# Batches of eight edge groups in a graph layer's gathers, the last chunk of the last group first

## The chip, the cores and the metric

The kernel runs on one core of a Trainium2 chip. The metric is the device time of one execution in microseconds (us); a profiled execution gives the rows of the trace. Engines: PE is TensorE (matmuls; PEld is its weight loads), DVE is VectorE, ACT is ScalarE, POOL is GpSimd, SP is SyncE.

## The reference

A graph layer over 12,500 nodes of 128 features and 200,000 edges, which come sorted by destination. Cut to what matters:

```python
hn = relu(layernorm(x))
w = edge_weight / max(segment_sum(edge_weight, dst), EPS)[dst]
feat = relu(hn @ W_pool + b_pool)
neigh = segment_max(feat[src] * w[:, None], dst)          # 0 for nodes without edges
h = relu(rownorm(hn @ W1_self + neigh @ W1_neigh + b1))
neigh2 = segment_sum(h[src] * w[:, None], dst) / max(deg, 1)
out = x + relu(h @ W2_self + neigh2 @ W2_neigh + b2)
```

So each edge needs a row of `feat` in the first pass and a row of `h` in the second, picked by its source node.

## The kernel before

The edges are cut into NG = 391 groups of G = 512, each of four chunks of P = 128 rows (the last group has 320 edges, three chunks). One chunk is one indirect DMA that GpSimd issues: `gather` (L502, the instruction at L507) makes four of them for a group, each picks 128 rows of 512 bytes out of a table in DRAM and puts them into one quarter of a buffer of 128 x 512 floats.

After a first stage that builds `feat_d` (its first 17 groups are gathered from x and treated apart), **pass 1** is one loop over the groups (L866 on; the gather is called at L877). In step i PE transposes the four chunks of group i into PSUM tile `pm` (L896), DVE multiplies them by the weights `gs` (L940), a step later it scans along the edges for the maximum (L911, with `kt` telling where a destination begins), copies (L933, L936) and picks the columns that end a destination (`sel`, L922). PE turns these back (`pr`, L952) and a product with `sel` (`pn`, L961) puts them into a window of nodes. About every four groups 128 nodes are complete; the node stages (L742 on) make h of them with PE, DVE and ACT and store it to `h_d`.

**Pass 2** (the loop after L1050, the gather at L1052) needs no transposes: DVE compares the edges' places (L996) and weighs them into `s` (L1001), PE multiplies each chunk by its part of `s` into `pa` (L1008, the chunks in reversed order, so the last chunk is read first), and DVE adds `pa` into the window of nodes (L1013). Each group has one L940 in pass 1 and one L1013 in pass 2. Nodes are finished about every four groups again. Groups 0 to 2 of this pass are gathered ahead.

The buffers come from `buffer`. At first there is a ring of 18 (some lent by other tables), then one of 14, and from group 113 of pass 1 on, and in all of pass 2, a ring of RING + MORE = 11 buffers called `full` (gt_98 to gt_108 in the listings). So a gather into a buffer waits until PE has read the group that stood in it before, which is eleven groups back in the ring of eleven. This wait is on PE's semaphore. Each gather has also a wait on its own lane of DMA completions (DMASW0 to DMASW7, eight lanes). The order of the instructions on each engine is the order of the code (a manual schedule); GpSimd does nearly nothing but gathers in the two passes. SP's queue loads `gs` for each group and `kt` for each four, DVE and ACT read the windows' places into registers for eight groups (BL = 8) at a time.

Of the kernel before, what the change touches and what calls it, by code (L numbers as in the profile page):

```python
# [18 lines left out]
P = 128  # L19
# [24 lines left out]
ADDED = PART_AT[-1] + PART  # L44
SCRATCH = 8192
MORE = 3


@with_exitstack
def gnn_kernel(ctx, tc, x, src, dst, ew, w_pool, b_pool, w1s, w1n, b1, w2s, w2n, b2, out):  # L50
# [20 lines left out]
    NG = GF + 1  # L71
# [7 lines left out]
    feat_d = dram.tile([NP, D], F32, name="feat_d")  # L79
    h_d = dram.tile([NP, D], F32, name="h_d")  # L80
# [40 lines left out]

    full = [gp.tile([P, Q, D], F32, name=f"gt{k}") for k in range(RING + MORE)]
    ring = full[:RING]
# [8 lines left out]
    def buffer(g, wide):  # L132
        if not wide:
            return full[g % len(full)]
        if WIDE <= g < WIDE + 3:
            k = g - WIDE
            return (work(f"f{k}").rearrange("p (q d) -> p q d", d=D) if k < 2 else ewT[:, 1])
        h = g if g < WIDE else g - 3
        if h < LESS:
            return ring[h % WIDE]  # L140
        return mid[(h - LESS) % MID] if h < LEAST else full[(h - LEAST) % len(full)]
# [36 lines left out]
    def strided(a, t, n):  # L178

        t0 = t - t % n  # L180
        return a[:, t0 * P:(t0 + n) * P].rearrange("d (p q) -> d q p", q=n)[:, t % n, :]
# [71 lines left out]
    def work(name, n=G, dtype=F32):  # L253
        return rp.tile([P, n], dtype, name=f"r_{name}")
# [242 lines left out]
    def edges_of(g):  # L497

        ne = G if g < GF else TAIL
        return *divmod(g, P), ne, [(j, min(P, ne - j * P)) for j in range(-(-ne // P))]  # L500

    def gather(gt, table_d, g, only=None, last=None):  # L502

        t, r, ne, chunks = edges_of(g)
        limit = {} if last is None else dict(bounds_check=last, oob_is_err=False)
        for j, k in chunks if only is None else chunks[only:only + 1]:
            nc.gpsimd.indirect_dma_start(  # L507
                out=gt[:k, j, :], out_offset=None, in_=table_d[:, :],
                in_offset=bass.IndirectOffsetOnAxis(ap=srcT[:k, t, j, r:r + 1], axis=0), **limit)
        return gt  # L510


    gts = {}
    raws = {}

    def raw_stats(r):
        mv = rp.tile([P, Q, 2], F32, name="raw_mv", bufs=3)
        for q in range(Q):
            st = rp.tile([P, 6], F32, name="raw_st", bufs=2)
            nc.vector.bn_stats(st, gts[r][:, q, :])  # L520
            nc.vector.bn_aggr(mv[:, q, :], st)  # L521
        rstd = rp.tile([P, Q], F32, name="raw_rstd", bufs=3)
        nc.scalar.activation(rstd, mv[:, :, 1], AF.Sqrt, bias=eps)
        raws[r] = mv, rstd
# [80 lines left out]
    for i in range(len(groups) + 3):  # L605
# [50 lines left out]
        while raw_chunks and 1 <= i <= 17:  # L656
            r, j = raw_chunks[0]
            if r >= WIDE - NT and i < 15 or r > WIDE - 3 and i < 17 or i < 9 and len(raw_chunks) <= Q * FIRST - 3 * i:
                break
            gts[r] = gather(buffer(r, True), x, r, only=j)  # L660
            raw_chunks.pop(0)
# [5 lines left out]
        k = i - len(groups)  # L667
# [29 lines left out]
    def pairs_of(g):  # L697

        t, r, ne, _ = edges_of(g)
        return t, r, ne, [(j, min(P, ne // 2 - j * P)) for j in range(-(-ne // (2 * P)))]  # L700
# [4 lines left out]
    def wide2(t):  # L705
        return Q if t < NF // Q * Q else 1
# [18 lines left out]
    def window_at(engine, g):  # L725

        if g % BL == 0 or engine not in held:
            lo = g // BL * BL
            _, held[engine] = nc.values_load_multi_w_load_instructions(
                bases[0:1, lo:min(lo + BL, NG)], [engine], min_val=0, max_val=N - 1,  # L730
                skip_runtime_bounds_check_because="destinations of edges are nodes, as the gathers have it")
        return held[engine][g % BL]
# [13 lines left out]
    def linear_own(po, t, self_w, n=1):  # L746
        nc.tensor.matmul(po, strided(turned_to[self_w], t, n), W[self_w], start=True, stop=False)
# [36 lines left out]
    def x_rows(wk, t, n, bufs):  # L784
        xr = wk.tile([P, n, D], F32, name=f"xr{n}", bufs=bufs)
        if n > 1:
            nc.sync.dma_start(in_runs(xr, n), runs(x, t, n, n))
        else:
            (q, p, view), = rows_of(x, t, 1)
            nc.sync.dma_start(xr[:p], view)  # L790
        return xr

    def nodes2(wk, ps, t, n, nT, xr):

        po = linear(ps, t, n, nT, "2s", "2n", b2_all)
        yield
        (q, p, view), = rows_of(out, t, 1)
        if t % n == 0:
            together["o"] = wk.tile([P, n, D], F32, name=f"o{n}", bufs=2)
        all_o = together["o"]  # L800
        o, xr = all_o[:p, t % n, :], xr[:p, t % n, :]
        nc.vector.scalar_tensor_tensor(o, po[:p, :], 0.0, xr, op0=OP.max, op1=OP.add)
        if n == 1:
            nc.sync.dma_start(view, all_o[:p])
        elif t % n == n - 1:
            nc.sync.dma_start(runs(out, t + 1 - n, n, n), in_runs(all_o, n))

    def stages(steps):
        for _ in steps:
            pass  # L810


    with tc.manual_schedule(), tc.tile_pool(name="ew", bufs=3) as wk, \
# [26 lines left out]
        def due(k):  # L840

            return i - k if 0 <= i - k < NG else None
# [23 lines left out]
        for i in range(max(turn) + 6):  # L866
# [7 lines left out]
            if i % KEPT == 0 and i and i + 2 < NG:  # L874
                keep_rows(i + 2, keep_tile())
            if FIRST <= i < NG:
                gts[i] = gather(buffer(i, True), feat_d, i)  # L877

            if i + 1 < NG:
                weight_rows(i + 1, wk.tile([P, G], F32, name="gs"))  # L880
# [12 lines left out]
            elif i < NG:  # L893
                gt = gts.pop(i)
# [5 lines left out]
            g = due(3)  # L900
            if g is not None:
                t, r, ne, chunks = pairs_of(g)
# [4 lines left out]
            g = due(1)  # L907
# [6 lines left out]
            if due(3) is not None:  # L914
                t, r, _, chunks = pairs_of(due(3))
# [31 lines left out]
            g = due(2)  # L947
# [7 lines left out]
            g = due(4)  # L955
            if g is not None:
                chunks = pairs_of(g)[3]
# [19 lines left out]
        i = NG  # L977
        side_step()
        for e in range(EARLY):
            gather(early[e], h_d[:(HI - LATE) * P], e, last=(HI - LATE) * P - 1)  # L980


    with tc.manual_schedule(), tc.tile_pool(name="ew2", bufs=3) as wk, \
# [10 lines left out]
        def places(g):  # L994
            t, r, _, _ = edges_of(g)
            nc.vector.tensor_tensor(hit, iota, locT[:, t, :, r:r + 1].to_broadcast([P, Q, PART]), OP.is_equal)  # L996

        def weighted(g):
            t, r, _, _ = edges_of(g)
            ss[g] = wk.tile([P, Q, PART], F32, name="s")  # L1000
            nc.vector.tensor_tensor(ss[g], hit, w2T[:, t, :, r:r + 1].to_broadcast([P, Q, PART]), OP.mult)  # L1001

        def window_product(g):
            chunks = edges_of(g)[3]
            pas[g] = ps.tile([P, ADDED], F32, name="pa", bufs=3)
            gt, s = gts.pop(g), ss.pop(g)
            for j, k in reversed(chunks):
                nc.tensor.matmul(pas[g][:, PART_AT[j]:PART_AT[j] + PART], gt[:k, j, :], s[:k, j, :],  # L1008
                                 start=j == len(chunks) - 1, stop=j == 0, skip_group_check=True)

        def window_add(g, at):
            n = ADDED if g < GF else PART_AT[len(edges_of(g)[3]) - 1] + PART
            nc.vector.tensor_tensor(agg2[:, bass.ds(at, n)], pas.pop(g)[:, :n], agg2[:, bass.ds(at, n)], OP.add)  # L1013
# [35 lines left out]
        first_groups = early_groups()  # L1049
        for i in range(max(turn) + 2):  # L1050
            if EARLY <= i < NG:
                gts[i] = gather(buffer(i, False), h_d, i)  # L1052
                places(i)
            if EARLY <= i < NG:
                weighted(i)
            if i + 4 in turn:
                n = turn[i + 4]
                if n % wide2(n) == 0:
                    xr = x_rows(wk, n, wide2(n), 2)
                xrs[n] = xr  # L1060
            if late is not None:
                stages(late)
                late = None
            if i in turn:
                n = turn[i]
                late = nodes2(wk, ps, n, wide2(n), strided(agg2, n, wide2(n)), xrs.pop(n))
                next(late)
            g = i - 1
            if EARLY <= g < NG:
                window_product(g)  # L1070
            if i >= EARLY and i % 2:
                next(first_groups, None)
            if i == NG - 1:
                for n in (HI - 2, HI - 1):
                    own[n] = flip[:, 0] if n % 2 else ps.tile([P, Q, D], F32, name="pl", bufs=1)[:, 0]
                    linear_own(own[n], n, "2s")
            g = i - 2
            if EARLY <= g < NG:
                window_add(g, window_at(mybir.EngineType.DVE, g))
# [18 lines left out]
    with tc.If(flag > 0):  # L1098
        with tc.tile_pool(name="gt", bufs=1) as tp, tc.tile_pool(name="gw", bufs=2) as wk, \
# [10 lines left out]
            for t0, n in node_groups():  # L1110
                c = slice(t0 * P, (t0 + n) * P)
                k = n * P
# [89 lines left out]
```

## Time and profile before

| | |
|---|---|
| three runs | 4612.95, 4617.0, 4617.24 us |
| median | 4617.0 us |
| profiled execution | 4650.7 us, its span 4648.7 us |
| mean granted clock of PE | 0.527 |
| gathers from `feat_d` into gt, 944 ns each | 1303 |
| gathers from `h_d` into gt, 944 ns each | 1551 |

A row of a table by stretches gives from:to and length in us, then for each engine (PE, PEld, DVE, ACT, POOL) the busy time and the number of instructions, the granted clock, the DMA engines' busy share and GB/s; of a single line of the kernel it gives only that line's engine. A row of the timeline gives start, duration, engine, line, operation, and in brackets the engine's idle time before it and what ended it; "issue" is time in which it waited for nothing that the profile shows, "remote" is a releaser that the profile cannot name. A row of waits gives total, times and longest.

### The profile page before, as it was taken

What the parts mean: (1) busy time and instruction counts of PE and PEld (TensorE: products, weight loads), DVE (VectorE), ACT (ScalarE), POOL (GpSimd) and SP (SyncE); (2) the same over time, 40 slices, a digit from 0 to 9 for tenths busy, and PEclk for the clock granted to TensorE, in tenths of its full rate; (3) what the DMA queues carried; (4) which work ended last, traced back from release to release, by engine and by line L of the source; (5) the groups of instructions that cost most, each with busy time, mean ns of one, the idle gap of its engine ahead of it and who ended that gap; (6) DMA issues with size and microseconds to landing.
All of it is one profiled execution on the core that took longest, in us unless ns stands there. A gap on an engine that the chain in (4) does not pass through costs nothing.

```text
span 4648.7 us, 32678 instructions
## 1 busy us (share of the span) xinstructions
PE 1995.1 (43%) x8700; PEld 1817.3 (39%) x8700; DVE 1741.8 (37%) x5165; ACT 416.0 (9%) x1509; POOL 2953.3 (64%) x3143
## 2 busy tenths in 40 slices
PE   3654543444444444444453344334334333334334
PEld 2444433443434343433342334333334333333334
DVE  3676655765666566665560111111101111111111
ACT  3531111111111111111110000000000000000000
POOL 5356666666666666666646666666666666666665
PEclk8665555555555555555555555555555555555555
DMA  4333443444444444444431112112111111211111
GB/s 130 109 114 116 126 117 103 125 117 114 118 115 120 115 117 116 119 116 117 113 100 46 47 47 62 51 50 56 50 52 53 51 52 51 55 51 52 53 54 45
DMA packets 196303, 397.11 MB, mean 85 GB/s; under 512 B 60703, under 2 KB 69790, under 8 KB 196112
## 3 DMA queue, kind: packets, MB, share of 16 engines
q0 software_dynamic: 100032, 204.97, 17.3%
q1 hardware_dynamic: 95344, 189.06, 13.2%
q8 instruction: 73, 1.20, 0.1%
q10 hardware_dynamic: 736, 0.92, 0.1%
q14 instruction: 118, 0.97, 0.1%
HBM read 374.96 MB, written 19.77 MB: 85 GB/s over the span
## 4 chain that ended last, share of the span: by engine, by line
another core or an unknown queue 23%; issue 23%; PE 20%; POOL 19%; DVE 13%; DMA 1%; ACT 1%; POOLq 0%; ACTq 0%; DVEq 0%
POOL gt L507 18%; PE pa L1008 5%; PE pm L896 5%; DVE pm L911 4%; PE pn L961 4%; DVE pm L940 2%; PE pr L952 2%; DVE sc L936 1%; DVE sc L933 1%; DMA gt<-h_d,srcT 1%; DVE sel L922 1%; PE pn L743 1%; PE pf L643 1%; PE pn L780 1%
## 5 line engine op out<-in xcount | busy, mean ns | idle before, releaser
L507 POOL DMA_INDIRECT gt<-h_d,srcT x1551 | 1463.9, 944 | 743.6 <-issue 419.6
L507 POOL DMA_INDIRECT gt<-feat_d,srcT x1303 | 1230.0, 944 | 680.5 <-issue 294.5
L1008 PE MATMUL pa<-s,gt 128*128 128x24 f32 x3102 | 685.3, 382 | 734.4 <-remote 561.1
L1008 PEld LDWEIGHTS pa<-s,gt 128*128 128x128 f32 x3102 | 682.0, 330 | 748.7 <-remote 567.8
L1013 DVE TENSOR_TENSOR way<-pa,way 128x41 f32 x391 | 78.0, 199 | 1866.9 <-remote 1323.6
L896 PE MATMUL pm<-ident,gt 128*128 128x128 f32 (+1 forms) x1303 | 349.7, 423 | 521.5 <-issue 314.3
L940 DVE TENSOR_TENSOR pm<-pm,gs 128x512 f32<-128x512 f32 x390 | 271.1, 695 | 694.6 <-remote 529.1
L911 DVE TENSOR_TENSOR_SCAN pm<-kt,carry,pm 128x512 f32<-128x512 bf16 x389 | 496.3, 1276 | 4.0
L961 PEld LDWEIGHTS pn<-sel,rows 128*128 128x128 f32 x1564 | 368.8, 324 | 230.8 <-ACT way L849 128.2
L896 PEld LDWEIGHTS pm<-ident,gt 128*128 128x128 f32 (+1 forms) x1303 | 235.8, 218 | 560.4 <-issue 338.5
L961 PE MATMUL pn<-sel,rows 128*128 128x48 f32 x1564 | 358.2, 377 | 217.4 <-ACT way L849 121.9
L743 PE MATMUL pn<-w_2n,way 128*128 128x128 f32 x192 | 74.4, 491 | 601.3 <-issue 325.9
L743 PEld LDWEIGHTS pn<-w_2n,way 128*128 128x128 f32 x192 | 52.8, 323 | 620.2 <-issue 406.6
L906 ACT ACTIVATE rows<-pr 128x256 f32<-128x256 f32 x392 | 149.7, 383 | 1532.8 <-remote 662.1
L952 PE MATMUL pr<-ident,sc 128*128 128x128 f32 x782 | 241.8, 411 | 8.0 <-issue 3.9
L922 DVE TENSOR_SCALAR sel<-cols,lastT,invT 128x48 f32<-128x48 f32 x782 | 243.6, 312 | 0.0
L933 DVE COPY sc<-pm 128x256 f32<-128x256 f32 x391 | 162.6, 416 | 109.5 <-remote 85.9
L952 PEld LDWEIGHTS pr<-ident,sc 128*128 128x128 f32 x782 | 167.2, 224 | 11.5 <-issue 6.1
L936 DVE COPY_PREDICATED sc<-kt,pm 128x256 f32<-128x256 int16 x389 | 168.5, 433 | 4.9 <-issue 4.9
L507 POOL DMA_INDIRECT w2T<-feat_d,srcT x100 | 94.3, 943 | 105.8 <-DVE raw_mv L521 52.0
L780 PE MATMUL pn<-ident,h 128*128 128x128 f32 x94 | 41.9, 446 | 236.8 <-DVE ss L765 73.0
L780 PEld LDWEIGHTS pn<-ident,h 128*128 128x128 f32 x94 | 17.3, 184 | 270.1 <-issue 217.2
(273 smaller groups left out, 2079.6 us busy)
## 6 DMA issues: line engine op xcount, KB each, us to landing
gs<-in_edge_weight SPq DMA_DIRECT2D x389, 256.0 KB
kt<-keep_d SPq DMA_DIRECT2D x97, 512.0 KB
gt<-h_d,srcT POOLq DMA_INDIRECT x1551
gt<-feat_d,srcT POOLq DMA_INDIRECT x1303
feat_d<-fr SPq DMA_DIRECT2D x24, 256.0 KB
xr<-in_x SPq DMA_DIRECT2D x24, 256.0 KB
out<-o SPq DMA_DIRECT2D x24, 256.0 KB
h_d<-h SPq DMA_DIRECT2D x47, 128.0 KB
```

Source lines behind the costliest of these rows:

```text
L507: nc.gpsimd.indirect_dma_start(out=gt[:k, j, :], out_offset=None, in_=table_d[:, :], in_offset=bass.IndirectOffsetOnAxis(ap=srcT[:k, t, j, ...
L743: nc.tensor.matmul(po, nT, W[neigh_w], start=False, stop=True)
L896: nc.tensor.transpose(pms[i][:, j * P:j * P + k], gt[:k, j, :], ident[:k, :k])
L906: nc.scalar.activation(rws[g][:k, j, :], pr[:k, j, :], AF.Copy)
L911: nc.vector.tensor_tensor_scan(pm[:, :ne], kt[:, :ne], pm[:, :ne], carry, op0=OP.add, op1=OP.max)
L922: nc.vector.tensor_scalar(part, cols[:k, 1, :], lastT[:k, t, j, r:r + 1], invT[:k, t, j, r:r + 1], op0=OP.is_equal, op1=OP.mult)
L933: nc.vector.tensor_copy(sc[:, :ne // 2], two[:, :, 1])
L936: nc.vector.copy_predicated(sc[:, :ne // 2], new[:, :, 1], two[:, :, 0])
L940: nc.vector.tensor_tensor(pms[i][:, :n], rows[:, :n], ws.pop(i)[:, :n], OP.mult)
L952: nc.tensor.transpose(prs[g][:k, j, :], sc[:, j * P:j * P + k], ident)
L961: nc.tensor.matmul(pas[g], rows[:k, j, :], sel[:k, j, :], start=j == 0, stop=j == len(chunks) - 1)
L1008: nc.tensor.matmul(pas[g][:, PART_AT[j]:PART_AT[j] + PART], gt[:k, j, :], s[:k, j, :], start=j == len(chunks) - 1, stop=j == 0, skip_group ...
```

## The change

Groups are now gathered in batches of BATCH = 8. At the head of a batch that begins at group g, the last chunk of the batch's last group, g + 7, is gathered first, into that group's buffer; then come the groups in order, and the last group leaves its last chunk out, since it is there. In pass 1 batches begin at group 128 (P), so there are 32 of eight and one of seven (384 to 390); in pass 2 they begin at group 16, so there are 46 of eight and the same one of seven. The number of gathers and their sizes are as before.

```diff
+BATCH = 8
...
-    def gather(gt, table_d, g, only=None, last=None):
+    def gather(gt, table_d, g, only=None, last=None, less=0):
...
-        for j, k in chunks if only is None else chunks[only:only + 1]:
+        for j, k in chunks[:len(chunks) - less] if only is None else chunks[only:only + 1]:
...
+    def gather_batched(wide, table_d, g, first):
+
+        if g >= first and (g - first) % BATCH == 0:
+            last = min(g + BATCH, NG) - 1
+            if last > g:
+                gather(buffer(last, wide), table_d, last, only=len(edges_of(last)[3]) - 1)
+        ahead = g >= first and ((g - first) % BATCH == BATCH - 1 or g == NG - 1) and (g - first) % BATCH > 0
+        return gather(buffer(g, wide), table_d, g, less=1 if ahead else 0)
...
-                gts[i] = gather(buffer(i, True), feat_d, i)
+                gts[i] = gather_batched(True, feat_d, i, P)
...
-                gts[i] = gather(buffer(i, False), h_d, i)
+                gts[i] = gather_batched(False, h_d, i, 2 * BATCH)
```

What the compiled program then holds on GpSimd, at three places. The first is in pass 1, before: the gathers of groups 248 and 249 (buffers gt_101 and gt_102 of the ring of eleven), each row with the semaphores that it waits for.

```order
1007 L507 DMA gt_100<-feat_d,srcT 128x128 [waits DMASW6_49,PE_49]
1008 L507 DMA gt_100<-feat_d,srcT 128x128 [waits DMASW7_49,PE_49]
1009 L507 DMA gt_101<-feat_d,srcT 128x128 [waits DMASW0_49,PE_49]
1010 L507 DMA gt_101<-feat_d,srcT 128x128 [waits DMASW1_49,PE_49]
1011 L507 DMA gt_101<-feat_d,srcT 128x128 [waits DMASW2_49,PE_49]
1012 L507 DMA gt_101<-feat_d,srcT 128x128 [waits DMASW3_49,PE_49]
1013 L507 DMA gt_102<-feat_d,srcT 128x128 [waits DMASW4_49,PE_49]
```

Each of the 32 gathers of eight groups waits for PE. The same place now, where group 248 heads a batch whose last group, 255, has buffer gt_108:

```order
1007 L508 DMA gt_100<-feat_d,srcT 128x128 [waits DMASW6_49]
1008 L508 DMA gt_100<-feat_d,srcT 128x128 [waits DMASW7_49]
1009 L508 DMA gt_108<-feat_d,srcT 128x128 [waits DMASW0_49,PE_49]
1010 L508 DMA gt_101<-feat_d,srcT 128x128 [waits DMASW1_49]
1011 L508 DMA gt_101<-feat_d,srcT 128x128 [waits DMASW2_49]
1012 L508 DMA gt_101<-feat_d,srcT 128x128 [waits DMASW3_49]
1013 L508 DMA gt_101<-feat_d,srcT 128x128 [waits DMASW4_49]
```

The gather into gt_108 has moved up to the head and holds the wait for PE; the 31 others wait for their lane alone. The second place is in pass 2, before, where gt_102 to gt_104 are the buffers of three groups in a row:

```order
1640 L507 DMA gt_102<-h_d,srcT 128x128 [waits DMASW7_49,PE_49]
1641 L507 DMA gt_102<-h_d,srcT 128x128 [waits DMASW0_49]
1642 L507 DMA gt_102<-h_d,srcT 128x128 [waits DMASW1_49]
1643 L507 DMA gt_102<-h_d,srcT 128x128 [waits DMASW2_49]
1644 L507 DMA gt_103<-h_d,srcT 128x128 [waits DMASW3_49,PE_49]
1645 L507 DMA gt_103<-h_d,srcT 128x128 [waits DMASW4_49]
```

Here one gather of each group waits for PE, the first. Now, from the last rows of one batch (its last group has buffer gt_99, with three chunks left) into the head of the next (whose last group has gt_107):

```order
1671 L508 DMA gt_98<-h_d,srcT 128x128 [waits DMASW6_49]
1672 L508 DMA gt_98<-h_d,srcT 128x128 [waits DMASW7_49]
1673 L508 DMA gt_99<-h_d,srcT 128x128 [waits DMASW0_49,PE_49]
1674 L508 DMA gt_99<-h_d,srcT 128x128 [waits DMASW1_49]
1675 L508 DMA gt_99<-h_d,srcT 128x128 [waits DMASW2_49]
1676 L508 DMA gt_107<-h_d,srcT 128x128 [waits DMASW3_49,PE_49]
1677 L508 DMA gt_100<-h_d,srcT 128x128 [waits DMASW4_49]
1678 L508 DMA gt_100<-h_d,srcT 128x128 [waits DMASW5_49]
```

Two gathers of a batch wait for PE, the head and the first of the last group's other three (since PE reads the last chunk of a group first in this pass, the head's wait does not cover the rest of that buffer). The third place is not changed: before, groups 121 to 123 of pass 1, whose buffers gt_106 to gt_108 are used there for the first time; row 513 is group 124.

```order
508 L507 DMA gt_107<-feat_d,srcT 128x128 [waits DMASW3_49]
509 L507 DMA gt_108<-feat_d,srcT 128x128 [waits DMASW4_49]
510 L507 DMA gt_108<-feat_d,srcT 128x128 [waits DMASW5_49]
511 L507 DMA gt_108<-feat_d,srcT 128x128 [waits DMASW6_49]
512 L507 DMA gt_108<-feat_d,srcT 128x128 [waits DMASW7_49]
513 L507 DMA gt_98<-feat_d,srcT 128x128 [waits DMASW0_49,PE_49]
514 L507 DMA gt_98<-feat_d,srcT 128x128 [waits DMASW1_49,PE_49]
```

The twelve gathers of these groups (rows 501 to 512) wait for no PE before the change either.

## The prediction

> **What bounds the kernel now.** I read the page first: the busy table, the groups, then GpSimd's waits.
>
> ```profile
> span 4648.7 us, 32678 instructions
> PE 1995.1 (43%) x8700; PEld 1817.3 (39%) x8700; DVE 1741.8 (37%) x5165; ACT 416.0 (9%) x1509; POOL 2953.3 (64%) x3143
> ...
> L507 POOL DMA_INDIRECT gt<-h_d,srcT x1551 | 1463.9, 944 | 743.6 <-issue 419.6
> L507 POOL DMA_INDIRECT gt<-feat_d,srcT x1303 | 1230.0, 944 | 680.5 <-issue 294.5
> ```
>
> The waits on GpSimd, from the view of waits:
>
> ```profile
> POOL gt L507 <- issue: 722.1, 2361, 1.8
> POOL gt L507 <- remote: 470.1, 224, 7.5
> POOL gt L507 <- PE pm L896: 104.1, 81, 22.8
> ```
>
> POOL is the busiest engine, and no engine is full. Most of its idle time before gathers (722 of some 1,420 us) is "issue", 0.3 us at a time between two gathers; the rest comes before some 300 gathers and is put down to "remote" (a releaser that the profile could not name) and to PE. By the code every buffer is released by PE (transposes L896, products L1008), so I take both for waits on PE. The next view is a table by stretches: the two long stretches in which the ring of eleven buffers is in use.
>
> ```profile
> 1000.00:2300.00 1300.00, 587.42 (x2570) 523.98 (x2570) 783.24 (x1957) 163.62 (x696) 848.83 (x901) 0.52 0.42 116
> 2500.00:4600.00 2100.00, 820.25 (x3616) 790.68 (x3615) 255.39 (x1222) 0.00 (x0) 1390.95 (x1475) 0.50 0.19 52
> ```
>
> Its columns are PE, PEld, DVE, ACT, POOL (busy, and how many), the granted clock, the DMA share and GB/s. The same table for one instruction that stands once in each group, the multiplication L940 in pass 1 and the addition L1013 in pass 2, counts groups:
>
> ```profile
> 766.80:779.00 12.20, 2.25 (x4) 0.50 0.48 131
> 779.00:801.90 22.90, 0.53 (x1) 0.50 0.29 77
> 801.90:824.60 22.70, 4.18 (x6) 0.58 0.30 90
> 1000.00:2300.00 1300.00, 155.82 (x224) 0.52 0.42 116
> ...
> 3546.80:3559.00 12.20, 1.19 (x6) 0.50 0.19 49
> 3559.00:3585.00 26.00, 0.20 (x1) 0.50 0.18 48
> 2500.00:4600.00 2100.00, 74.40 (x373) 0.50 0.19 52
> ```
>
> Pass 1 takes 1300 / 224 = 5.80 us per group, pass 2 2100 / 373 = 5.63. Four gathers need less. GpSimd's own rows around the longest stall, and in two ordinary places:
>
> ```profile
> 767.28 0.94 POOL L507 DMA_INDIRECT gt<-feat_d,srcT  x1 [1.77 <-PE pr L952]
> 768.53 0.94 POOL L507 DMA_INDIRECT gt<-feat_d,srcT  x1 [0.31 <-issue]
> ...
> 787.25 0.95 POOL L507 DMA_INDIRECT gt<-feat_d,srcT  x1 [0.30 <-issue]
> ...
> 800.98 0.94 POOL L507 DMA_INDIRECT gt<-feat_d,srcT  x1 [0.30 <-issue]
> 824.76 0.94 POOL L507 DMA_INDIRECT gt<-feat_d,srcT  x1 [22.84 <-PE pm L896]
> ...
> 871.25 0.94 POOL L507 DMA_INDIRECT gt<-feat_d,srcT  x1 [3.35 <-remote]
> ```
> ```profile
> 3547.07 0.94 POOL L507 DMA_INDIRECT gt<-h_d,srcT  x1 [3.75 <-remote]
> 3586.21 0.94 POOL L507 DMA_INDIRECT gt<-h_d,srcT  x1 [4.48 <-remote]
> ...
> 3598.43 0.94 POOL L507 DMA_INDIRECT gt<-h_d,srcT  x1 [2.47 <-remote]
> ```
>
> From 767.28 to 800.98 lie 27 steps of 1.248 us, so a group costs POOL 4.99 us and a run of eight 39.9. POOL is therefore idle for 0.6 to 0.8 us per group, waiting for PE. So PE and DVE set the pace, though both are far from full. Why they are slow shows in three stretches around the 22.8 us stall:
>
> ```profile
> 766.80:779.00 12.20, 8.32 (x38) 7.55 (x37) 9.92 (x24) 1.67 (x7) 8.97 (x10) 0.50 0.48 131
> 779.00:801.90 22.90, 2.17 (x10) 2.17 (x11) 3.76 (x9) 0.97 (x5) 17.42 (x19) 0.50 0.29 77
> 801.90:824.60 22.70, 10.70 (x55) 9.31 (x54) 17.47 (x45) 5.17 (x19) 0.03 (x1) 0.58 0.30 90
> ```
>
> For some 12 us after POOL starts again everything runs: 38 matmuls. Then POOL gathers on at its even pace, and PE, DVE and ACT nearly stand still: 10 matmuls in 22.9 us. When POOL is idle they run again, 55 in 22.7 us. The clock was 0.50 in both of the first two, so it is not the clock. Pass 2 shows the same in the rows above: six groups in the first 12.2 us of a run, one in the next 26. And so do two stretches of the first stage, one with gathers back to back (10 in 12 us) and one with 6 in 62 us:
>
> ```profile
> 50.00:62.00 12.00, 0.40 (x2) 0.11 (x1) 0.00 (x0) 0.00 (x0) 9.24 (x10) 1.00 0.21 54
> 107.00:169.00 62.00, 56.88 (x231) 45.17 (x231) 46.29 (x207) 50.23 (x112) 5.42 (x6) 0.78 0.35 117
> ```
>
> I read this as: **gathers that run without a pause for longer than about 12 us starve PE, and a pause of POOL frees it.** Why, no view says. The stalls are then no mere loss, they are what lets PE work. I take this as the bound. The trace shows that they go together; which causes which is inferred, above all from the 20 us ahead of 801, where POOL waited for nobody.
>
> **The change, part by part.** The number of gathers, their sizes and their 944 ns stay. Four things move.
>
> *Waits that go.* In a run of eight groups the order of POOL's instructions (shown with the change) leaves PE waits at one gather of pass 1 and two of pass 2, from 32 and 8. What such a wait costs by itself: the gathers from 787.25 to 800.98 are the twelve of groups 121 to 123, which even now wait for no PE, since they are the first into new buffers. They keep the same 0.30 us as those ahead of them. So I cost the waits removed at 0; the other bound is what the idle of 0.30 could lose at most, which the twelve exclude.
>
> *The chunk moved forward.* At a head one gather of 1.248 us goes ahead of the next group's four, so this group is complete 1.248 us later. No cost while PE has older groups to work on, at most 1.248 us in a run of eight otherwise. In pass 1 three landed groups hold PE for 3 x 3.6 us (rows below), longer than the 7.2 us that the next group takes, so 0 there (else 32.9 x 1.248 = 41 us); in pass 2 it stands in the sum below. Behind the waiting head on POOL's queue stand only the 31 other gathers of the run, and for them waits PE; SP's loads and the register loads of DVE and ACT do not pass it.
>
> *The condition.* Before, a gather of group g waits for PE to have read group g - 11. Now the head waits for g + 7 - 11 = g - 4, and then eight groups go without a pause. PE may be ten groups behind when POOL runs on before, and three now. The first head of each pass waits for seven groups more, once; at the pass's end those seven are already done, so this comes back, and I count 0 for it (if not, 7 x 3.5 = 25 us).
>
> *The rhythm.* This is the sum. Pass 1 now: 4 groups in a cycle of about 4 x 5.80 = 23.2 us, four of them by the row 766.80:779.00 in its first 12.2 us; the slow rest and the 3.35 us stall yield nearly none. So the rule gives the present pace. With the change a run lasts 39.9 us: four groups in its first 12.2 us, one in the other 27.7 (row 779.00:801.90: one in 22.9), and the three others have to come out of POOL's idle time. How long three take there, the 22.7 us of idle show, with these multiplications:
>
> ```profile
> 806.89 0.70 DVE L940 TENSOR_TENSOR pm<-pm,gs 128x512 f32<-128x512 f32 x1 [16.52 <-remote]
> ...
> 810.67 0.70 DVE L940 TENSOR_TENSOR pm<-pm,gs 128x512 f32<-128x512 f32 x1
> ...
> 814.19 0.70 DVE L940 TENSOR_TENSOR pm<-pm,gs 128x512 f32<-128x512 f32 x1
> ```
>
> The first comes 5.0 us after POOL's last gather, each next one some 3.6 us later: 5.0 + 2 x 3.6 = 12.2. The cycle is 39.9 + 12.2 = 52.1 against 8 x 5.80 = 46.4, **+5.7 us**. There are 32 runs of eight and one of seven, 32.9: **+188 us**. Lower bound: the first group after 3.35 us as in the row at 871.25, 50.4, +4.0, +132 us. Upper: none in the slow part, four to come, 55.7, +9.3, +306 us.
>
> Pass 2: 8 x 5.63 = 45.0 us now. With three landed groups at a head, the fourth's last gather ends 6 x 1.248 - 0.3 = 7.2 us after the release and the fifth's at 12.2, so the first 12.2 us hold four groups where the row 3546.80:3559.00 has six. With one in the slow part five are done, three are left for the idle time. The first takes 3.57 us (mean of 3.75, 4.48 and 2.47), each next 12.2 / 6 = 2.0: 7.6. The cycle is 47.5, +2.5; 46 runs and one of seven, 46.9: **+117 us**. Lower bound: seven done as now, one left: 39.9 + 4.5 = 44.4, -0.6, -28 us. Upper: four done, four left, first after 4.48: 50.4, +5.4, +253 us. I take the middle because the three-group limit follows from the order.
>
> Together +188 + 117 = **+305 us**, bounds +104 and +559. The profiled execution took 4650.7 us, 2.0 outside its span and 0.7% above the median of the three runs, 4617.0. Differences of this size carry over, so 4617 + 305 = **4922**, between 4721 and 5176. A difference of 0.2% (9 us) is about what a measurement of this kernel can tell from none.
>
> **The rivals.**
>
> *A stall has a fixed price (faster).* Every stall ends with PE's releases coming together; if a stall frees PE by itself, however long the run before, one stall of about 4.5 us per eight groups would do: 39.9 + 4.5 = 44.4. Pass 1: -2.0 x 32.9 = -66 us; pass 2: -0.6 x 46.9 = -28; 4617 - 94 = 4523. For it: the stalls of pass 2 come after longer runs than those of pass 1 and are little longer (4.48 after 39 us, 3.35 after 23). Against: 4.5 us hold one or two groups, and the head asks for all but three; after the run of 35 us ahead of 801.9 it took 22.8. That stall also had to give back three groups of lead (fourteen buffers became eleven, 3 x 3.6 = 10.8), which leaves 12.0. Chance 0.16. The Trainium skill (Perfetto Trace Analysis, Identifying the Most-Contended Engine) advises to find the engine with the highest occupancy and to work on that one first; here that is GpSimd, and by it fewer waits there should pay. The trace disagrees as far as it goes: in 779.00:801.90 GpSimd was as full as it can be, and one group came out.
>
> *PE and DVE have their own pace (no change).* If PE is slow for a reason of its own, and POOL merely stops when its ring is full, the pace of 5.80 and 5.63 stays and only the places of the stalls move: 4617, give or take 9. For it: PE sets the pace in both. Against: 231 matmuls in 62 us with few gathers, two in 12 us with many. Chance 0.08.
>
> *Less starving (a little slower).* If the head's long stall lengthens the good time behind it, only the heads' stricter condition costs: some 0 to 100 us, 4626 to 4721. Chance 0.09.
>
> That the change does not do what it says is excluded by the order: the PE waits stand where described.
>
> **How the numbers follow.** The forecast with its bounds (4721 to 5176) has 0.61, above it 0.06, a little slower 0.09, no change 0.08, faster 0.16. So slower 0.76, same 0.08, faster 0.16. For 8 in 10 the range leaves out the faster case and what lies above: 4608 (0.2% under the median) to 5176; the likeliest case alone is 4721 to 5176.
>
> **What would show it.** In the profile after: POOL runs of 32 gathers, 39.9 us each, and one stall per run of 8 to 16 us in pass 1 and 4 to 11 in pass 2, where now there are 2 to 5 us; four or so multiplications in the first 12 us of a run and one in the rest; PE's matmuls crowded into the stalls. Wrong would be: stalls under 6 us in pass 1 (then the fixed price is right), or PE running evenly through a run of 40 us, or a stall that is no shorter although PE ran (then the condition alone is it).

## The result and the profile after

The changed kernel took 4919.19 us, median of four runs (4914.75 to 4922.6), against 4614.98 us before (4604.09 to 4617.24): ratio 1.0664, 95% interval 1.0643 to 1.0684, so +304 us. Its profiled execution took 4922.6 us, the one of before 4650.7.

The top of the page of the changed kernel:

```profile
span 4920.7 us, 31357 instructions
PE 1999.2 (41%) x8700; PEld 1820.0 (37%) x8700; DVE 1739.6 (35%) x5165; ACT 422.4 (9%) x1509; POOL 2960.9 (60%) x3143
```

Every engine did the same work in nearly the same busy time; what grew is the idle time. Its waits on GpSimd:

```profile
POOL gt L508 <- issue: 824.8, 2706, 0.6
POOL gt L508 <- PE pm L907: 438.9, 38, 25.9
POOL gt L508 <- PE pa L1019: 215.1, 33, 17.0
POOL gt L508 <- PE pr L963: 94.2, 18, 15.9
POOL gt L508 <- remote: 93.0, 33, 5.9
```

The stalls are fewer and much longer, and now they name PE. Where the time went, the first and last start of the group counters shows, L940 (now L951) for pass 1 and L1013 (now L1024) for pass 2. First before, then after:

```profile
L940 DVE TENSOR_TENSOR pm<-pm,gs x390: 498/696/703, 174.8 to 2400.6; 128x512 f32<-128x512 f32 x195
L1013 DVE TENSOR_TENSOR way<-pa,way x391: 190/201/204, 2432.9 to 4639.9; 128x41 f32 x195, 128x33 f32 x1
```
```profile
L951 DVE TENSOR_TENSOR pm<-pm,gs x390: 497/695/700, 172.9 to 2662.5; 128x512 f32<-128x512 f32 x195
L1024 DVE TENSOR_TENSOR way<-pa,way x391: 186/201/203, 2692.6 to 4912.0; 128x41 f32 x195, 128x33 f32 x1
```

Pass 1 grew from 2225.8 to 2489.6 us (+263.8), pass 2 from 2207.0 to 2219.4 (+12.4). The profiled execution of before is 34 us above its median, so it makes the growth too small. A later trace in which pass 1 is as before (`p2_only` below) has 2204.1 us there, which makes it +285. One cycle of pass 1, the timeline of POOL in the changed kernel:

```profile
1518.26 0.95 POOL L508 DMA_INDIRECT gt<-feat_d,srcT  x1 [13.98 <-PE pr L963]
1519.51 0.95 POOL L508 DMA_INDIRECT gt<-feat_d,srcT  x1 [0.30 <-issue]
...
1557.03 0.94 POOL L508 DMA_INDIRECT gt<-feat_d,srcT  x1 [0.30 <-issue]
1571.89 0.94 POOL L508 DMA_INDIRECT gt<-feat_d,srcT  x1 [13.92 <-PE pm L907]
```

A run of 32 gathers, then a stall of 14 us, as the prediction drew it; over the 24 full cycles from 1078 us on the stall has 13.1 to 17.1 us, 14.9 in the mean. What the other engines do in that cycle (table by stretches; PE, PEld, DVE, ACT, POOL), and below it how many groups are multiplied in the same stretches:

```profile
1518.90:1535.00 16.10, 9.82 (x42) 8.55 (x42) 11.99 (x34) 2.44 (x9) 12.14 (x14) 0.50 0.57 157
1535.00:1558.80 23.80, 4.47 (x18) 3.96 (x18) 4.42 (x9) 0.49 (x2) 17.48 (x19) 0.50 0.26 63
1558.80:1573.20 14.40, 7.53 (x34) 7.16 (x34) 12.21 (x31) 3.93 (x16) 1.00 (x2) 0.50 0.34 108
```
```profile
1518.90:1535.00 16.10, 2.08 (x3) 0.50 0.57 157
1535.00:1558.00 23.00, 0.70 (x1) 0.50 0.27 65
1558.90:1573.20 14.30, 2.78 (x4) 0.50 0.33 107
1000.00:2600.00 1600.00, 162.70 (x234) 0.51 0.35 98
```

Three groups come in the first 16 us of the run, one in the other 23, four in the stall. A group takes 1600 / 234 = 6.84 us, a cycle of eight 54.7. Pass 2 in the changed kernel, the additions L1024 in two cycles that follow each other, and over 2000 us:

```profile
3503.60:3529.60 26.00, 1.40 (x7) 0.50 0.19 51
3529.60:3543.60 14.00, 0.00 (x0) 0.50 0.19 52
3543.60:3549.20 5.60, 0.40 (x2) 0.50 0.04 12
3548.80:3574.80 26.00, 0.81 (x4) 0.50 0.26 71
3574.80:3588.80 14.00, 0.00 (x0) 0.50 0.20 52
3588.80:3594.40 5.60, 0.59 (x3) 0.50 0.04 12
2867.00:4867.00 2000.00, 70.12 (x351) 0.50 0.20 52
```

In the first cycle seven groups come in the first 26 us, five of them in the first 10, then none for 14 us; in the next cycle four, then none for 14 us. Most cycles take turns in this way. Around these two cycles the stall is 5.5 to 5.9 us, and a group takes 2000 / 351 = 5.70 us.

### The profile page after: what moved, and what is told of

Read it like the earlier page. It is cut to its first block, busy times and chain, and to the rows that moved or that the text cites. A ratio compares the mean times of both kernels' runs of the same rounds, so it can differ in the third digit from the quotient of the medians.

```text
span 4920.7 us, 31357 instructions
## 1 busy us (share of the span) xinstructions
PE 1999.2 (41%) x8700; PEld 1820.0 (37%) x8700; DVE 1739.6 (35%) x5165; ACT 422.4 (9%) x1509; POOL 2960.9 (60%) x3143
## 3 DMA queue, kind: packets, MB, share of 16 engines
q1 hardware_dynamic: 95344, 189.06, 12.4%
## 4 chain that ended last, share of the span: by engine, by line
another core or an unknown queue 40%; PE 16%; DVE 16%; issue 15%; POOL 12%; DMA 1%; ACT 1%; DVEq 0%; ACTq 0%; POOLq 0%
POOL gt L508 12%; DVE pm L922 5%; PE pm L907 4%; PE pa L1019 3%; PE pn L972 3%; DVE pm L951 3%; PE pr L963 2%; DVE sc L947 1%; DVE sc L944 1%; DMA gt<-h_d,srcT 1%; DVE sel L933 1%; PE pn L754 1%; PE pn L758 1%; PE pf L654 1%
## 5 line engine op out<-in xcount | busy, mean ns | idle before, releaser
L1019 PE MATMUL pa<-s,gt 128*128 128x24 f32 x3102 | 705.8, 383 | 1025.9 <-DMA gt<-h_d,srcT 412.0
L1024 DVE TENSOR_TENSOR way<-pa,way 128x41 f32 x391 | 78.1, 200 | 1844.8 <-remote 1228.1
L951 DVE TENSOR_TENSOR pm<-pm,gs 128x512 f32<-128x512 f32 x390 | 270.9, 695 | 934.4 <-remote 723.3
L754 PE MATMUL pn<-w_1n,way 128*128 128x128 f32 x192 | 65.9, 446 | 265.4 <-issue 243.6
L754 PEld LDWEIGHTS pn<-w_1n,way 128*128 128x128 f32 x192 | 50.0, 319 | 275.9 <-issue 253.3
```

The source lines that it names most:

```text
L754: nc.tensor.matmul(po, nT, W[neigh_w], start=False, stop=True)
L951: nc.vector.tensor_tensor(pms[i][:, :n], rows[:, :n], ws.pop(i)[:, :n], OP.mult)
```

## The experiments

The runs were made on four chips, in four lots, each lot beside the kernel before on its own chip. On two of them (lots 1 and 4, and by its time the result above) the kernel before takes about 4615 us; on the other two (lots 2 and 3) it takes 3943. So a lot on the second kind of chip also shows what the change costs where PE is not starved.

Theory A: gathers that run back to back starve PE, which gets a portion of groups through per run of POOL, about four in pass 1 and six or seven in pass 2. Rival B: the head's stricter condition costs by itself. Rival C: PE and DVE have their own pace.

**Lot 1. Pass 1 alone.** The changed kernel, its pass 2 as before.

```diff
-                gts[i] = gather_batched(False, h_d, i, 2 * BATCH)
+                gts[i] = gather(buffer(i, False), h_d, i)
```

> Only pass 1 is batched, pass 2 is as before. Theory A (a run of gathers lets PE through a fixed amount of work, about four groups of pass 1 or six of pass 2, then PE nearly stops until POOL pauses): nearly the whole difference lies in pass 1, by the pitch of the changed kernel's profile (6.86 against 5.81 us per group, 263 groups: +276 us), so about 4890 us (4870 to 4910). The split of the prediction (+188 in pass 1): about 4803 us.

Measured 4907.24 us beside 4615.53, ratio 1.0634 (1.0616 to 1.0652): +292 us. Nearly all of the loss lies in pass 1, against the prediction's split.

**Lot 1. Pass 2 alone.** The changed kernel, its pass 1 as before.

```diff
-                gts[i] = gather_batched(True, feat_d, i, P)
+                gts[i] = gather(buffer(i, True), feat_d, i)
```

> Only pass 2 is batched. Theory A: six groups get through a run however they are spread, two are left for a stall of 5 to 6 us, 45.4 us a cycle: within 20 us of the kernel before, 4595 to 4635. The prediction's rule (PE stops 12 us after POOL starts again, whatever it has done; +117): about 4732 us.

Measured 4637.51 us, ratio 1.0042 (1.0026 to 1.0059): +22 us, just above what theory A expected and far from +117. The two parts add to 314, about the 304 of the whole.

**Lot 1. Without gathers.** The kernel before, its buffers from group 128 and 16 on left as they are; the rest of the work stays.

```diff
-                gts[i] = gather(buffer(i, True), feat_d, i)
+                gts[i] = gather(buffer(i, True), feat_d, i) if i < P else buffer(i, True)
...
-                gts[i] = gather(buffer(i, False), h_d, i)
+                gts[i] = gather(buffer(i, False), h_d, i) if i < 2 * BL else buffer(i, False)
```

> The kernel before, without the gathers of groups 128 and up in pass 1 and of groups 16 and up in pass 2: PE works on what lies in the buffers, the rest is as it was. Theory A (gathers starve PE): groups at 3.4 to 4.0 us in pass 1 and about 2.0 us in pass 2, 2600 to 2900 us in all. Rival C (PE and DVE have their own pace and POOL only waits for them): the pace of 5.8 and 5.65 us stays, about 4600 us.

Measured 2669.98 us in one run. The group counters, L940 and then L1013:

```profile
950.00:1700.00 750.00, 150.07 (x217) 0.56 0.38 119
...
1920.00:2620.00 700.00, 67.53 (x337) 0.50 0.05 17
```

That is 3.46 us per group in pass 1 and 2.08 in pass 2, where the kernel before has 5.80 and 5.63 on the same kind of chip. PE and DVE have no such pace of their own: rival C falls. Without gathers PE also has no rows to wait for, but late rows are not what holds it: in pass 1 of the changed kernel's trace the last DMA packet of a gather ends 1.1 to 3.8 us after GpSimd's instruction, and on a chip without starving (lot 3) 1.1 to 3.3.

**Lot 1. A pause in mid-run.** The changed kernel, with six index fills on GpSimd before the fifth group of each run of pass 1.

```diff
+                if i > P and i % BATCH == BATCH // 2:
+                    pause(6)          # six nc.gpsimd.iota into a tile of 128 x 512
                 gts[i] = gather_batched(True, feat_d, i, P)
```

> The changed kernel, with six index fills of 128 x 512 on GpSimd (about 3.4 us together) in the middle of each run of pass 1, so that POOL issues no gather for that time. Theory A: the pause gives PE a second portion of four groups, the stall at the head falls from 14.7 us to 3 to 6 us, a cycle from 54.9 to 46 to 49 us: 4630 to 4730 us. Rival B (the head's condition by itself costs the time): the run gets 3.4 us longer and the stall as much shorter, about 4919 us. The same if work on GpSimd that is not a gather is no pause to PE.

Measured 4737.47 us, ratio to the kernel before 1.026 (1.0241 to 1.0278), 182 us less than the changed kernel took in the result (the kernel before had 4615 us in both); just above what theory A expected. GpSimd's timeline over one cycle, the fills and the gathers that stood idle before:

```profile
1516.63 3.71 POOL L520 IOTA idle<- 128x512 f32 x6
1520.49 0.96 POOL L508 DMA_INDIRECT gt<-feat_d,srcT  x1 [0.15 <-issue]
...
1544.55 0.94 POOL L508 DMA_INDIRECT gt<-feat_d,srcT  x1 [5.62 <-PE pm L915]
...
1565.52 3.72 POOL L520 IOTA idle<- 128x512 f32 x6
...
1590.08 0.94 POOL L508 DMA_INDIRECT gt<-feat_d,srcT  x1 [2.21 <-remote]
```

3.7 us more work on GpSimd shorten the head's stall from 13 to 17 us to between 1.3 and 6.6 at 18 of the last 28 heads of pass 1 (five had none, five still 12.7 to 20.1), and the kernel gets faster. Rival B, for which the pause only fills waiting time, has no place for a gain; the pause leaves the head's condition as it is. It also shows that GpSimd need not be idle: work there that is no gather serves as well.

**Lot 2. Batches of four.**

```diff
-BATCH = 8
+BATCH = 4
...
-                gts[i] = gather_batched(False, h_d, i, 2 * BATCH)
+                gts[i] = gather_batched(False, h_d, i, 4 * BATCH)
```

> The changed kernel with batches of four groups: one wait for PE per 16 gathers of pass 1, the head waits for group g - 8 in place of g - 4, a run lasts 20 us. Theory A (a portion of about four groups of pass 1, six of pass 2, per run of POOL): a run of four groups uses up one portion, as before the change, so 4600 to 4680 us. Rival B (the stricter condition costs by itself, the more the fewer groups of lead are left: ten, seven, three): somewhere half way, 4700 to 4830 us.

Measured 3944.63 us beside 3943.04, ratio 1.0005 (0.9995 to 1.0015). Neither range was met, since on this chip the question did not arise: no gather waited for PE longer than the usual 0.3 us between two gathers, as its waits on GpSimd show.

```profile
POOL gt L508 <- issue: 756.0, 2483, 0.3
POOL gt L508 <- DMA gt<-h_d,srcT: 34.7, 114, 0.3
POOL gt L508 <- PE pa L1019: 21.3, 70, 0.3
POOL gt L508 <- PE pm L907: 16.8, 55, 0.3
```

**Lot 2. A short pause for each group, and a longer one for each four.** In the kernel before, one fill ahead of each group (first), or four ahead of each fourth (second).

```diff
+                if i >= P and i % 1 == 0:        # second kernel: i % 4 == 0, pause(4)
+                    pause(1)
                 gts[i] = gather(buffer(i, True), feat_d, i)
...
+                if i >= 2 * BL and i % 1 == 0:   # second kernel: as above
+                    pause(1)
                 gts[i] = gather(buffer(i, False), h_d, i)
```

> The kernel before with one index fill of 0.56 us on GpSimd ahead of each group's four gathers, from group 128 of pass 1 and 16 of pass 2 on. POOL alone then needs 5.55 us per group. If many short pauses serve PE as well as a long one: 5.55 us in both passes, about 4510 us. If a pause must last 2 us or more to free PE: portions and stalls are as before and the fills come on top, 0.5 us for each of 640 groups, 4850 to 4990 us.

> The same with four fills (2.2 us) ahead of each fourth group. If 2.2 us are enough to free PE: 5.55 us per group, about 4510 us. If PE needs 2.5 to 4 us of POOL without a gather, the fills only stand in for a part of the stall that comes anyway: 4600 to 4680 us; if they come in the wrong place, up to 4850.

Measured 4231.38 us (ratio 1.0731, 1.0713 to 1.0749) and 4321.35 (1.096, 1.0942 to 1.0978). Without starving there is nothing to free, and the fills add to GpSimd's time: +288 and +378 us, or about 0.45 and 0.59 us for each of some 640 fills. The ranges expected were for a chip that starves. Whether short pauses help on a chip that starves is left open.

**Lot 2. A quarter of the bytes.** The kernel before; each gather fetches 128 rows of 128 bytes, of other rows, so the sums are of other numbers.

```diff
-                out=gt[:k, j, :], out_offset=None, in_=table_d[:, :],
+                out=gt[:k, j, :d], out_offset=None, in_=table_d[:, :] if d == D else table_d[:, :].rearrange("n (q d) -> (n q) d", d=d),
...
-                gts[i] = gather(buffer(i, True), feat_d, i)
+                gts[i] = gather(buffer(i, True), feat_d, i, d=D if i < P else D // 4)
...
-                gts[i] = gather(buffer(i, False), h_d, i)
+                gts[i] = gather(buffer(i, False), h_d, i, d=D if i < 2 * BL else D // 4)
```

> The kernel before, where from group 128 of pass 1 and 16 of pass 2 on a gather fetches 128 rows of 128 bytes in place of 512 (a quarter of each row, and of other rows; so the sums are of other numbers). The number of gathers and of rows stays. If the bytes moved starve PE: POOL's 4.99 us become the pace, about 4180 us. If it is the gathers as such: 5.8 and 5.65 us as before, 4550 to 4650 us.

Measured 3943.12 us in one run beside 3943.04: on this chip GpSimd's pace is the time, and the bytes do not matter to it.

**Lot 3. The changed kernel and the batches of four again.**

> The changed kernel once more, beside the kernel before on the same chip, since the kernel before took 4615 us in the runs up to here and 3943 us in the last four, where POOL never waited for PE. If the kernel before takes about 3943 us here, PE is not starved, three landed groups are enough (theory A: the change costs only by starving) and the change makes no difference: 3935 to 3955 us. Rival B (the head's condition costs by itself): one stall at each head, 80 heads of 1 to 5 us, 4020 to 4340 us. If the kernel before takes about 4615 us, as the first time, 4900 to 4930 us.

> Batches of four groups, the head waits for group g - 8. Where the kernel before takes about 4615 us: by theory A a run of 20 us uses up one portion as before the change, 4600 to 4680 us; by rival B half way to the changed kernel, 4700 to 4830 us. Where the kernel before takes about 3943 us: the same as it, as in the run before.

Once more a chip where the kernel before takes 3943.44 us. The changed kernel took 3944.83 us, ratio 1.0005 (0.9996 to 1.0015), the batches of four 3946.22, the same ratio and interval. The changed kernel's page, its waits and its pace there (L951, then L1024):

```profile
span 3941.1 us, 31357 instructions
PE 2100.8 (53%) x8700; PEld 1785.7 (45%) x8700; DVE 1757.5 (45%) x5165; ACT 419.4 (11%) x1509; POOL 2954.0 (75%) x3143
```
```profile
POOL gt L508 <- issue: 791.7, 2600, 0.3
POOL gt L508 <- DMA gt<-h_d,srcT: 20.4, 67, 0.3
POOL gt L508 <- DMA gt<-feat_d,srcT: 17.1, 56, 0.3
POOL gt L508 <- PE pm L907: 15.2, 50, 0.3
```
```profile
900.00:1900.00 1000.00, 140.57 (x201) 0.51 0.47 135
...
2150.00:3850.00 1700.00, 68.72 (x342) 0.50 0.21 60
```

The same program, the same 944 ns gathers, nearly the same granted clock (0.51 and 0.50), and a group takes 4.98 and 4.97 us, which is four gathers. PE keeps up with gathers that never pause, the head's wait for group g - 4 finds it done, and the change is worth nothing either way. So the head's condition costs nothing by itself, and rival B falls. On a chip that starves, the longer run and the stricter condition come together; the pause in mid-run, which leaves the condition, won back 182 of the 304 us, and batches of four, meant to part the two, never met such a chip.

**Lot 4. Without gathers, and a quarter of the bytes, again.**

> The kernel before without most of its gathers, once more. Theory A (only gathers starve PE, and only on some chips): 2640 to 2700 us whatever the kernel before takes on this chip, as in the first look (2669.98 us, beside 4615). If a chip that takes 3943 us with gathers is faster in PE or DVE as such: about 0.85 of it, 2280 us.

> Gathers of 128 rows of 128 bytes in place of 512 (of other rows, so the sums are of other numbers), from group 128 of pass 1 and 16 of pass 2 on. Where the kernel before takes 4615 us: if the bytes moved starve PE, about 4180 us; if the gathers as such do, 4550 to 4650 us. Where it takes 3943 us: POOL's pace as before, 3943 us.

The kernel before took 4613.31 us here. Each kernel of this lot was timed once. Without gathers 2675.67, as on the other such chip. With a quarter of the bytes 4611.71; its counters, L940 and then L1013:

```profile
1000.00:2300.00 1300.00, 157.52 (x226) 0.52 0.31 84
...
2500.00:4500.00 2000.00, 71.47 (x358) 0.50 0.09 18
```

5.75 and 5.59 us per group, as with whole rows. So it is not the bytes that starve PE; what does is there whatever the rows' length.

## Why the prediction was right

The forecast was 4922 us, +305; measured +304. The mechanism held, two terms of its sum were off in opposite directions, and that the sum fell so near is chance.

*What bounds the kernel.* The prediction inferred from stretches with and without gathers that gathers starve PE and that a pause frees it. Leaving the gathers out showed the first (3.46 and 2.08 us per group against 5.80 and 5.63), the pause in mid-run the second. It did not see that this is so on some chips alone. Its 4615 us kernel is a 3943 us kernel elsewhere, with GpSimd's pace as the bound.

*Removed waits at 0.* Where nothing starves this is right: the waits go and the time stays (ratio 1.0005). On a chip that starves no run parts them from the rest. The rule of the Trainium skill that was weighed (Perfetto Trace Analysis, Identifying the Most-Contended Engine: look after the busiest engine first) fits that chip, where GpSimd is 75% busy and its 4.99 us are the time, but even there the waits were not what kept it.

*Pass 1, +188 us; measured +264 by the profile, +285 with the later trace, +292 alone.* The term that was too small is what is left for the stall. The prediction gave a run four groups in its first 12.2 us and one in the rest, and left three. Counted over the 24 full cycles, a run has 3.0 groups in its first 12.2 us and 1.3 in the rest, so 3.7 are left. The prices were about right: in the cycle above the first group of the stall is multiplied 2.4 us after the last gather's end (5.0 taken; 1.0 to 5.4 over the cycles), the next ones 3.1 to 3.7 us apart (3.6 taken), in the timeline of DVE:

```profile
1560.39 0.70 DVE L951 TENSOR_TENSOR pm<-pm,gs 128x512 f32<-128x512 f32 x1 [19.30 <-remote]
1564.08 0.69 DVE L951 TENSOR_TENSOR pm<-pm,gs 128x512 f32<-128x512 f32 x1
1567.14 0.69 DVE L951 TENSOR_TENSOR pm<-pm,gs 128x512 f32<-128x512 f32 x1
1570.33 0.69 DVE L951 TENSOR_TENSOR pm<-pm,gs 128x512 f32<-128x512 f32 x1
```

The cycle is 54.7 us where 52.1 was forecast, inside its bounds of 50.4 and 55.7; with 39.7 us from the first gather's start to the last one's end, that is a stall of 14.9.

*Pass 2, +117 us; measured +12 by the profile, +22 alone.* The step that failed is the count of groups that a run lets through. The prediction had four in the first 12.2 us and one in the slow rest, five in all, the same in every run, so that three are left for a stall of 7.6 us. Over 43 full runs it is 4.4 and 1.5, and 2.1 are left for a stall of 6.0 us in the mean. The runs are not alike: 17 of them let eight groups through and 20 let four, mostly by turns, as in the two cycles above. So neither "only the first 12 us" nor a fixed number of groups per run describes it. Why they take turns is open; no run tested it.

*The rivals.* A fixed price per stall (4523 us) fell with stalls of 14 us in pass 1; in pass 2 it comes near, with one stall of mostly 5.2 to 6 us for each eight groups where it took 4.5. An own pace of PE (no change) fell with the run without gathers. The condition alone, asked for as what would show the prediction wrong, fell with lot 3.

*Left open.* What in a gather starves PE, why two chips of the four lots show it and two do not, whether many short pauses would help, and batches of four on a chip that starves: both lots with that kernel were on chips of the other kind. No version that does all the work was found to beat the kernel before on either kind of chip.

One lead stands in the traces. Engines and DMAs release each other by semaphore updates, and a trace records them. Each gather ends with 16 packets of four bytes, so 16 updates are due, 50,016 for the 3126 gathers in a trace. Lot 3's trace of the changed kernel has 49,949 of them, the result's trace of the same program 6745. In lot 1's run without gathers, 1052 of 8192 are there up to 900 us, while GpSimd still gathers; from 950 to 1700 us, with no gather, none of the DVE's 1831 updates or the 4768 of other DMAs is missing. So on the chips that starve, what carries these updates or their records falls behind just while gathers run. That this holds the engines up is not shown. Nor is it shown that PE itself stands still: the transposes of the group multiplied at 1560.39 are shown at 1541.2 to 1542.3 us with modelled ends, and either they or their updates came late. Every timed run of the four lots has a span and a clock from the profiler, so no run excludes the rival that it is the recording that slows these chips.

## What to carry to other kernels

A stall is not always a loss: before merging waits into fewer and longer runs, count what the other engines get done inside the stalls and inside the runs, in stretches of some ten microseconds. If an engine with free time stands still while another runs, leave that other's work out once and see; one such run tests what a profile can only suggest. Read more than one cycle before taking a cycle as the rule: in pass 2 the neighbour of the first one shown has four groups where it has seven. And run the kernel before beside the kernel after on more than one chip where a bound looks odd: here the same pair differs by 6.6% on one and by nothing on the next.

## What the runs showed of the hardware

The kernel before took 4604 to 4623 us on some chips (4650.7 in the execution profiled first) and 3940 to 3946 us on others, at granted clocks of about 0.52 on both kinds. On the first kind, gathers of 128 rows issued every 1.248 us brought the rows of PE, DVE and ACT to a near stop after some 12 to 25 us of pass 1 (one group in 23 us of the cycle shown). The first group after the last gather of a run came 1.0 to 5.4 us after its end. With rows of 128 bytes in place of 512 the pace was the same (5.75 and 5.59 us per group). Six index fills (3.7 us) on GpSimd in mid-run took 182 us off the changed kernel. On the second kind nothing of this appeared, with gathers that never paused (4.98 and 4.97 us per group). The traces of the first kind hold 6745 of the gathers' 50,016 semaphore updates in the changed kernel, those of the second 49,949.
